# Working image by image, with convolution, projections and second layer issued in small steps between the pieces of a selective scan, and half of the C products on GpSimd

## The chip, the cores and the metric

The kernel runs on one core of a Trainium2 chip. The metric is the time of one execution on the device in microseconds, lower is better. Executions of one kernel agree within about 0.3 %. All runs quoted here were undisturbed ("fast").

## The reference, cut to what matters

The input is four images of 64 x 64 positions with 96 channels, in fp32. Layer 0 is a convolution block with binary weights and a selective scan in four directions; layer 1 is linear attention and a feed-forward net with quantised values.

```
x  = x + layer0(groupnorm(x))
     # 96 -> 192+192 channels (x, z), 3x3 convolution, silu, four scan directions of 192 channels x 16 states:
     dA = exp(dt[..., None] * A)                     # the "decay"
     h  = dA * h + (dt * u)[..., None] * Bt          # the recurrence; (dt*u)*B is the "inject"
     y  = einsum('bkdn,bkn->bkd', h, Ct)             # "C product" and sum over the 16 states
     # four directions added, layernorm over channels, gated by z, projected back to 96
t  = tokens(x)
t  = t + attention(layernorm(t))                     # no softmax: k and v reduce to one small matrix
t  = t + ffn(layernorm(t))                           # 96 -> 384 -> 96, fp8 products
```

## The kernel before

Two images form a pair. For each pair the kernel runs a front (`prologue`: input projection, convolution, projections of B, C and dt), then the scans, then a back (`epilogue`: directions, layernorm, gate). The second layer comes at the very end. Only the softplus of dt (`prepare`) runs between the scans.

```
    for pr in range(NB // 2):
        ...
            prologue(tc, a, pr, gT, c)
            scans(tc, pr, gT, c)
        epilogue(tc, a, pr, c)
    layer1(tc, a, x1d, out, ident, eps5, hmask)
```

The scans of all images are 1536 pieces of 128 rows (32 channels x 4 states) by 1024 positions. A piece passes through five operations on four engines: a decay on ScalarE (into PSUM), an inject on GpSimd, the scan on VectorE, the C product on GpSimd or VectorE, and a reduction on TensorE (four matmuls in the trace) that sums over the states into a PSUM bank `y`.

```
        bcp, dlp, sw, pw, yw = pool("sbc", 6), pool("sdl", 3), pool("sw", 8), pool("spw", 2), pool("syw", 2)
        ps_a, ps_b = pool("sps", 2, space=PSUM), pool("spb", 2, space=PSUM)
        ...
        def pooled(i):
            return i % 8 in (0, 3, 5)
        ...
        def scan(i):
            ...
            h = w if pooled(i) else dA
            nc.vector.tensor_tensor_scan(
                h, dA, w, 0.0 if ci == 0 else carries[u][:, g, q : q + 1], ALU.mult, ALU.add
            )
            if pooled(i):
                carry(i, h)                                   # a ScalarE copy of the last column
                nc.gpsimd.tensor_tensor(w, h, cr, ALU.mult)
            else:
                nc.vector.tensor_tensor(w, h, cr, ALU.mult)
                carry(i, h)
        ...
        for i, (u, ci, g, q) in enumerate(pieces):
            ...
            decay(i + 1)
            inject(i + AHEAD)                                 # AHEAD = 4
            scan(i)
            if i % 8 == 2 and i > 8:
                evacuate(i - 3)                               # copies the bank of eight sums out
            if i >= 1:
                reduce(i - 1)
            ...
            advance()                                         # one step of softplus
```

## Time and profile before

The kernel takes 7612.65 us (median of the four runs on one chip, 7603.54 to 7622.04). The lines of its profile are shown and added up in the prediction below. In the list of costliest groups, a line gives the source line, the engine, the operation, what it writes and reads, the count, then total busy time and mean nanoseconds of one, and last the idle time just before it with what ended it. The outcome: 5093 us of the profiled execution are scans with two full engines, and 2492 us are other work in which those two engines have little to do.

### The profile page before, as it was taken

What the parts mean: (1) busy time and instruction counts of PE and PEld (TensorE: products, weight loads), DVE (VectorE), ACT (ScalarE), POOL (GpSimd) and SP (SyncE); (2) the same over time, 40 slices, a digit from 0 to 9 for tenths busy, and PEclk for the clock granted to TensorE, in tenths of its full rate; (3) what the DMA queues carried; (4) which work ended last, traced back from release to release, by engine and by line L of the source; (5) the groups of instructions that cost most, each with busy time, mean ns of one, the idle gap of its engine ahead of it and who ended that gap; (6) DMA issues with size and microseconds to landing.
All of it is one profiled execution on the core that took longest, in us unless ns stands there. A gap on an engine that the chain in (4) does not pass through costs nothing. (4 is left out here: it accounts for less than half of the span.)

```text
span 7584.7 us, 48672 instructions
## 1 busy us (share of the span) xinstructions
PE 4209.9 (56%) x14531; PEld 1204.3 (16%) x14531; DVE 5865.7 (77%) x4026; ACT 3108.1 (41%) x4634; POOL 5004.0 (66%) x2226
## 2 busy tenths in 40 slices
PE   4996455555555444435799455555555544442756
PEld 2233100000000000002324210000000000000344
DVE  1112799999999999987212299999999999996877
ACT  2124455555554433422313355555555444441323
POOL 0000799999999999950000099999999999993012
PEclk8557556666666666657558566666655566665867
DMA  2001566654666444443100356655567544445111
GB/s 49 33 17 63 186 187 168 184 184 165 186 179 166 158 144 154 142 182 83 44 34 9 124 175 179 180 175 184 181 168 179 171 155 147 151 148 192 47 25 32
DMA packets 750581, 1010.17 MB, mean 133 GB/s; under 512 B 521875, under 2 KB 522444, under 8 KB 743756
## 3 DMA queue, kind: packets, MB, share of 16 engines
q1 hardware_dynamic: 750316, 1007.07, 44.1%
q8 instruction: 114, 1.87, 0.1%
q14 instruction: 151, 1.24, 0.1%
HBM read 812.17 MB, written 188.48 MB: 132 GB/s over the span
## 5 line engine op out<-in xcount | busy, mean ns | idle before, releaser
L524 POOL TENSOR_TENSOR w<-dl,bc 128x1024 f32<-128x1024 f32 x1536 | 3584.3, 2373 | 1360.7 <-DMA dl<-dld 1291.3
L561 PE MATMUL yp<-w,sum 128*32 128x512 f32 x6144 | 2417.8, 985 | 2584.7 <-POOL w L546 2379.8
L516 ACT ACTIVATE dA<-dl,anm 128x1024 f32<-128x1024 f32 x1536 | 1715.6, 1117 | 667.7 <-DVE w L548 474.7
L541 DVE TENSOR_TENSOR_SCAN dA<-dA,carry,w 128x1024 f32<-128x1024 f32 x720 | 1688.1, 2345 | 62.4 <-ACT dA L516 31.3
L546 POOL TENSOR_TENSOR w<-w,bc 128x1024 f32<-128x1024 f32 x576 | 1362.4, 2366 | 132.3 <-ACT carry L533 107.8
L548 DVE TENSOR_TENSOR w<-dA,bc 128x1024 f32<-128x1024 f32 x960 | 1176.0, 1225 | 83.8 <-DVE dA L541 1.4
L561 PEld LDWEIGHTS yp<-w,sum 128*32 128x32 f32 x6144 | 351.9, 146 | 4422.9 <-POOL w L546 3155.7
L541 DVE TENSOR_TENSOR_SCAN w<-dA,carry,w 128x1024 f32<-128x1024 f32 x432 | 1011.3, 2341 | 0.0
L533 ACT COPY carry<-dA 128x1 f32<-128x1 f32 x720 | 114.7, 159 | 1666.5 <-DVE w L548 1666.5
L541 DVE TENSOR_TENSOR_SCAN dA<-dA,w 128x1024 f32<-128x1024 f32 x240 | 548.8, 2287 | 32.5 <-ACT dA L516 19.2
L311 DVE TENSOR_SCALAR t<-t,pv 128x512 f32<-128x512 f32 x48 | 23.3, 486 | 610.8 <-ACT t L307 610.8
L541 DVE TENSOR_TENSOR_SCAN w<-dA,w 128x1024 f32<-128x1024 f32 x144 | 328.3, 2280 | 48.5 <-POOL w L524 48.0
L296 PE MATMUL cvps<-tp,cw 128*128 128x512 bf16 (+1 forms) x576 | 358.0, 622 | 2.5 <-ACT u L275 2.5
L299 PE MATMUL cvps<-tp,cw 64*128 64x512 bf16 (+1 forms) x576 | 356.5, 619 | 0.0
L269 POOL MEMSET tp<- 128x4356 bf16 x6 | 22.1, 3726 | 485.3 <-ACT xsT L257 485.3
L651 PE MATMUL mu<-y,lnm 128*128 128x512 f32 x224 | 137.5, 756 | 272.8 <-DVE y L645 227.6
L356 DVE COPY xr<-tp 64x1536 bf16<-64x1536 bf16 x64 | 60.8, 949 | 293.9 <-PE tp L351 293.9
L775 POOL MEMSET tT<- 1x4096 f32 x4 | 14.0, 3506 | 406.1 <-PE zp L704 296.9
L442 PE MATMUL dps<-gT,wdz 48*128 48x64 bf16 (+1 forms) x2048 | 175.8, 310 | 92.7 <-ACT pd L464 91.7
L307 ACT ACTIVATE t<-cvps,cbias,csc 128x512 f32<-128x512 f32 x48 | 37.3, 777 | 443.3 <-PE cvps L299 443.3
L457 DVE TENSOR_TENSOR pd<-dps,pu 128x512 f32<-128x512 f32 x192 | 165.1, 860 | 55.2 <-DMA pu<-ud 47.1
L819 POOL CAST h<-h 128x512 fp8e5<-128x512 f16 x96 | 81.9, 867 | 190.0 <-DVE h L818 190.0
(174 smaller groups left out, 4329.2 us busy)
## 6 DMA issues: line engine op xcount, KB each, us to landing
dl<-dld SPq DMA_DIRECT2D x768, 512.0 KB
bc<-bcd SPq DMA_DIRECT2D x512, 512.0 KB
dld<-pd SPq DMA_DIRECT2D x64, 1024.0 KB
pu<-ud SPq DMA_DIRECT2D x96, 512.0 KB
yd<-ys SPq DMA_DIRECT2D x384, 128.0 KB
dld<-pd SPq DMA_DIRECT2D x64, 512.0 KB
yk<-yd SPq DMA_DIRECT2D x12, 2048.0 KB
ud<-u SPq DMA_DIRECT2D x12, 1024.0 KB
```

The costliest lines, as they stand in the source:

```text
L296: nc.tensor.matmul(ps[prow, :], c["cw0"][:, t, co], tpad[j][:, win[0], win[1]], start=(t == 0), stop=False)
L299: nc.tensor.matmul(ps[prow, :], c["cw1"][rows, t, co], tpad[2][rows, win[0], win[1]], start=False, stop=(t == 8),)
L442: nc.tensor.matmul(pv[rows, s], c["wdz"][:, k, s, ch], gT[:, k, h, :, c0 : c0 + 16], start=True, stop=True)
L457: nc.vector.tensor_tensor(d[:, 1, cols].rearrange("p (i j) -> p i j", j=64), ps.rearrange("p (i j) -> p i j", j=64), uv[:, 8 * hf : 8 * hf ...
L516: nc.scalar.activation(t, dlt[u, ci, g][0], AF.Exp, scale=c["anm"][:, units[u][0], g, q : q + 1])
L524: nc.gpsimd.tensor_tensor(t, dlt[u, ci, g][1], bct[u, ci, q][0], ALU.mult)
L533: nc.scalar.copy(carries[u][:, g, q : q + 1], h[:, CH - 1 : CH])
L541: nc.vector.tensor_tensor_scan(h, dA, w, 0.0 if ci == 0 else carries[u][:, g, q : q + 1], ALU.mult, ALU.add)
L546: nc.gpsimd.tensor_tensor(w, h, cr, ALU.mult)
L548: nc.vector.tensor_tensor(w, h, cr, ALU.mult)
L561: nc.tensor.matmul(y[at : at + 32, :], c["sum4"], prod[:, 512 * hf : 512 * hf + 512], start=(q == 0), stop=(q == NQ - 1), tile_position=(0 ...
L651: nc.tensor.matmul(ps, c["lnm"][:, m, :], src[s], start=(i == 0), stop=(i == len(terms[T]) - 1))
```

## The change

The intent is to let the 2492 us of other work run on TensorE and ScalarE while VectorE and GpSimd scan. For that the images are worked one at a time, all other stages are rewritten with channels on the partitions and cut into small generator steps, and one such step is issued per piece. Only the first image's front and the last image's back stay outside. To give VectorE room for the new steps, GpSimd takes half the C products in place of three in eight, and copies the carry of its own pieces. The diff is a rewrite of most of the file; its core:

```
+    def back():
+        yield from prologue(c, 1)
+        for b in range(NB):
+            if b + 2 < NB:
+                yield from prologue(c, b + 2)
+            while not scans[b].done(2):
+                yield
+            yield from turn(c, b)                  # sums of the two transposed directions
+            while not scans[b].done(NK):
+                yield
+            yield from epilogue(c, b)              # back of layer 0, and all of layer 1
...
-        bcp, dlp, sw, pw, yw = pool("sbc", 6), pool("sdl", 3), pool("sw", 8), ...
-        ps_a, ps_b = pool("sps", 2, space=PSUM), pool("spb", 2, space=PSUM)
+        gT=pool("gTp", 2), bc=pool("bcp", 5), dl=pool("dlp", 3), w=pool("wp", 7), y=pool("yp", 2),
+        dA=pool("dAp", 2, space=PSUM), ps=pool("psp", 1, space=PSUM),     # single banks for all sums
...
-            return i % 8 in (0, 3, 5)
+        return i % 2 == 0
...
+        if pool:
+            if ci < NCH - 1:
+                nc.gpsimd.tensor_copy(one, h[:, CH - 1 : CH])
+            nc.gpsimd.tensor_tensor(w, h, cr, ALU.mult)
...
+            if i >= 1:
+                self.reduce(i - 1)                 # still ahead of the step, as before
...
+            interleave(lanes)                      # one step of softplus
+            next(back, None)                       # one step of everything else
```

## The prediction

> **What bounds the kernel now.** I first read the occupancy in forty slices, because it shows whether the kernel is one regime or several.
>
> ```profile
> PE   4996455555555444435799455555555544442756
> DVE  1112799999999999987212299999999999996877
> POOL 0000799999999999950000099999999999993012
> ```
>
> The reader is to see two long stretches in which VectorE (DVE) and GpSimd (POOL) are both at 9, and three stretches (start, middle, end) in which GpSimd does nothing and VectorE little. TensorE is full only in two spots there. Next, the first and last scan instruction give the borders: scans run from 792 to 3338 us and from 4344 to 6891 us. Busy time by stretch then says what each regime is limited by (columns: stretch, length, busy us of PE, weight loads, DVE, ACT, POOL, TensorE clock, DMA share, GB/s):
>
> ```profile
> 171.00:560.00 389.00, 376.54 (x952) 102.87 (x952) 62.64 (x93) 74.43 (x93) 0.00 (x0) 0.54 0.07 25
> 792.00:3327.00 2535.00, 1261.61 (x3938) 230.58 (x3940) 2436.11 (x1412) 1213.53 (x1858) 2432.96 (x1053) 0.63 0.55 166
> 4300.00:6900.00 2600.00, 1287.27 (x4016) 236.72 (x4015) 2452.16 (x1427) 1229.92 (x1883) 2441.41 (x1056) 0.62 0.56 167
> 7100.00:7585.00 485.00, 307.93 (x1734) 206.43 (x1732) 363.06 (x509) 146.13 (x230) 95.86 (x100) 0.74 0.15 36
> ```
>
> So 2546 + 2547 = **5093 us are scans**, 1536 pieces at 3.32 us, with VectorE and GpSimd both 96% busy. The other 7585 - 5093 = **2492 us** are convolution, projections, normalisation and the second layer: 792 at the start, 1006 in the middle, 694 at the end, with the two scan engines mostly empty. The costliest groups give the price of a piece:
>
> ```profile
> L524 POOL TENSOR_TENSOR w<-dl,bc 128x1024 f32<-128x1024 f32 x1536 | 3584.3, 2373 | 1360.7 <-DMA dl<-dld 1291.3
> L561 PE MATMUL yp<-w,sum 128*32 128x512 f32 x6144 | 2417.8, 985 | 2584.7 <-POOL w L546 2379.8
> L516 ACT ACTIVATE dA<-dl,anm 128x1024 f32<-128x1024 f32 x1536 | 1715.6, 1117 | 667.7 <-DVE w L548 474.7
> L541 DVE TENSOR_TENSOR_SCAN dA<-dA,carry,w 128x1024 f32<-128x1024 f32 x720 | 1688.1, 2345 | 62.4 <-ACT dA L516 31.3
> L546 POOL TENSOR_TENSOR w<-w,bc 128x1024 f32<-128x1024 f32 x576 | 1362.4, 2366 | 132.3 <-ACT carry L533 107.8
> L548 DVE TENSOR_TENSOR w<-dA,bc 128x1024 f32<-128x1024 f32 x960 | 1176.0, 1225 | 83.8 <-DVE dA L541 1.4
> ```
>
> Of eight pieces three have their C product on GpSimd. GpSimd: 8 x 2.37 + 3 x 2.37 = 26.1 us, 3.26 a piece; VectorE: 8 x 2.34 + 5 x 1.225 = 24.9 us, 3.11 a piece, plus the softplus stage that runs between the scans (0.68 + 0.86 us x 192, 0.19 a piece) = 3.30. Both give the measured 3.32. Inside the scans GpSimd's own waits are small; the whole-run list of its waits has these:
>
> ```profile
> POOL w L524 <- DMA dl<-dld: 1291.3, 2, 648.3
> POOL w L546 <- ACT carry L533: 107.8, 122, 3.2
> POOL w L524 <- DMA bc<-bcd: 66.2, 55, 5.1
> ```
>
> The first is no DMA problem: two waits of 648 us, the stages ahead of each scan.
>
> **What the Trainium skill says.** "Perfetto Trace Analysis", Optimization Strategy: where the most-contended engine differs between regimes, interleaving the regimes can help. The slices above show such regimes, and the change does this. "GPSIMD Engine Reference", 3.1: a two-input elementwise operation costs GpSimd about 2.6 cycles per element at 1.2 GHz, some twice VectorE; 1024 elements would be 2.2 us, the trace has 2.37 against 1.225, so it agrees. "TensorE: Matmul & The Clock Gate", Engine queue depths: ScalarE, VectorE and GpSimd are strict FIFOs, and only weight loads overtake on TensorE. No row of this trace tests that, but it is what makes me charge for interleaving. The same page, on fp8: without the double-row mode it runs at bf16 speed; I therefore count no gain for the convolution's fp8. (The fp8 matmuls before, 0.47 us for 96x512 at another clock, do not contradict it.)
>
> **The change part by part.**
>
> *1. Only image 0's front and image 3's back stay outside.* The order of instructions says so: on VectorE 205 rows stand ahead of the first scan and 90 after the last; on GpSimd nothing but two products follows the last inject. The background generator takes one step per piece. I counted its steps: front 183, transposing two directions' sums 34, back 218. Fronts 1 and 2 fill pieces 0 to 366, image 0's back ends at piece 618, image 1's at 1053, image 2's at 1370; all this the VectorE order confirms. Image 3's back, 218 steps, can only start after piece 1536.
>
> *Start.* Constants and input until the convolution: 171 us before for two images, about 150 for one. Convolution: 16 tiles, each 18 matmuls x 0.615 us (L296/L299 at clock 0.5) = 11.1, one projection 0.5, two ScalarE reads of the single bank 1.55, so 13.2 x 16 = 211. Then 64 units of 12 transposes (0.106 each, busy time over count), a ScalarE copy (half of 1.59), six matmuls (0.16) and hand-overs: 3.3 x 64 = 211, plus 16 x 2.3 for signs and B/C = 37. Round trips through memory 25, eight softplus steps (92 us for twelve before) 60. Sum **about 695 us**, against 792: halving the images saves little because the new steps use single banks and run one after the other.
>
> *Tail.* First half of image 3's back, per 512 tokens: 22 fp32 matmuls of 1.0 us (L651: 244 us for 224), some two not on the path, other small matmuls 4, about a dozen ScalarE/VectorE steps of 0.65 us on the path 8, loads of 2 MB at some 190 GB/s 10: 42 us, x 8 = 336. Second half: 3 fp32 matmuls, fp8 matmuls, ten steps, load latency: 20 us x 8 = 160. **About 500 us**, against 694.
>
> *2. Half the C products on GpSimd.* GpSimd: 1536 + 768 = 2304 products. Back-to-back triples of injects in the timeline last 6.95 us, so 2.32 each: 5345 us. New are 576 carry copies of 128x1 on GpSimd (its 128x1 fills take 0.11 us; I take 0.2): 115. Sum **5460 us, 3.55 a piece, against 3.26**. VectorE: 1536 x 2.34 + 768 x 1.225 = 4535, plus softplus 256 x 1.5 = 390 and about 330 of other steps = 5255, 3.42 a piece. GpSimd becomes the bound. The carry wait (108 us) goes.
>
> *3. What interleaving costs in the scans.* (a) Convolution, 48 tiles: a tile takes four pieces, 4 x 3.55 = 14.2 us, but TensorE needs 11 + 0.5 + 4 x 1.57 (2417.8/1536 for the reductions) = 17.8 us, and the next decay queues on ScalarE behind a read that waits for it: about 4.5 us each, 215. (b) Back, first half, 24 blocks: TensorE 28 + 14 x 1.57 = 50 us in 14 pieces worth 50 us, unevenly spread: 6 each, 145. (c) Transposing units: 3.8 us of TensorE against 3.55: 0.4 x 200 = 80. (d) B/C buffers 6 to 5: the load for the second next tile goes out one piece later; waits for it from 66 to perhaps 200. Sum 640, of which a third should overlap: **+425 us**.
>
> Total: 695 + 5460 + 425 + 500 = **7080 us**.
>
> **The rivals.**
> *Everything hides.* Steps fall wholly into TensorE's and ScalarE's slack (TensorE is 50% busy in the scans, ScalarE 48%). Then 695 + 5460 + 500 = 6655. For it: before, softplus hid almost fully. Against it: the convolution stretch shows TensorE 97% busy for 389 us; that doesn't fit into half an engine without delay.
> *TensorE becomes the bound.* Its work in the scans sums to some 4600 us (2418 reductions, 540 convolution, 840 back, 800 the rest) of 5900, so not on average; but if each phase lost twice my charge (3a to 3d in full, doubled), the scans take 6700 and the total nears 7900: slower. Against it: reductions lag with four injects ahead and seven w buffers.
> *More work on GpSimd is itself a loss.* If GpSimd's copies cost 0.5 us and its products lengthen beside more VectorE traffic, 3.8 a piece, total 7450: no change within 2%.
>
> **Range and chances.** The sure gain is 2492 - 1195 = 1297 us of serial work; the sure cost is 367 us of scan bound; the unsure cost is 0 to 1200. For a gain below 2% the unsure cost must pass 800, nearly twice my estimate. Range 6750 to 7440; faster 0.85, same 0.10, slower 0.05.
>
> **What the changed profile would show.** First scan near 695, last near 6580. GpSimd at 9 in all slices between, product at 2.3 to 2.4 us, x768, carry copies near 0.2; if much above, step 2 is wrong. GpSimd's waits for the B/C load near 200 us (3d). Scans per us lower in the two convolution phases (pieces 30 to 100 and 215 to 285) than in pieces 1404 to 1536, which have only scans and should run at 3.6. TensorE about 75% in the scans. A tail of 450 to 550 us with no engine full. I would be wrong if phases show VectorE waiting on decays for most of the time, if the tail is memory-latency bound at 700, or if the products slow down.

## The result, and the profile after

The changed kernel is correct and takes 7545.59 us (median of four, 7530.09 to 7555.51). The ratio to the kernel before is 0.991 (95 % interval 0.9888 to 0.9932). A ratio here is the mean time of one kernel's fast runs over that of the other's fast runs of the same rounds, so it is not quite the ratio of the medians. The gain is 0.9 %, and the prediction had 7 %.

Busy tenths in forty slices of the kernel after:

```profile
PE   3745678767976776566777677556557765654684
DVE  1106786788676779988757677988867789888401
POOL 0007787888787778898868778888988789999500
```

The empty stretch in the middle is gone, as intended. But GpSimd now stands at 7 and 8 where it stood at 9, and VectorE falls to 5 and 6 in places. Only near the end, where no background is left, it stays at 9.

Busy time by stretch (columns as in the prediction: stretch, length, busy us of PE, weight loads, DVE, ACT, POOL, TensorE clock, DMA share, GB/s), for the scans and the tail:

```profile
597.00:7083.00 6486.00, 4342.56 (x15056) 1355.04 (x15058) 5126.24 (x3211) 3391.29 (x4985) 5455.16 (x2904) 0.69 0.55 156
7083.00:7548.00 465.00, 320.24 (x640) 117.02 (x636) 49.71 (x89) 118.62 (x203) 0.00 (x0) 0.66 0.21 52
```

Start 597, scans 6486, tail 465. The start was predicted at 695 and the tail at 500, so both came out better. The scans were predicted at 5460 + 425 = 5885. They are 601 us longer, which is more than the whole miss of 466 us. GpSimd is 84 % busy in them (5455 of 6486 us).

The groups that answer to those of before:

```profile
L849 POOL TENSOR_TENSOR w<-dl,bc 128x1024 f32<-128x1024 f32 x1536 | 3594.7, 2356 | 1319.6 <-DMA dl<-dld 586.8
L883 PE MATMUL yp<-w,sum 128*32 128x512 f32 x6144 | 2331.0, 873 | 1692.3 <-POOL w L868 1119.1
...
L868 POOL TENSOR_TENSOR w<-w,bc 128x1024 f32<-128x1024 f32 x768 | 1804.6, 2350 | 110.1 <-DVE w L864 62.2
L864 DVE TENSOR_TENSOR_SCAN dA<-dA,carry,w 128x1024 f32<-128x1024 f32 x576 | 1351.5, 2346 | 356.9 <-ACT dA L842 242.5
```

No operation of the scan became slower: injects 2356 ns (2373 before), C products 2350 (2366), scans 2346 (2345). What grew is idle time. This scan group waited 356.9 us in 576 pieces; before, the like group waited 62.4 us in 720. The list of waits says on whom (engine, tile, line, what it waits for, total us, times, longest):

```profile
PE yp L883 <- POOL w L868: 1119.1, 339, 33.5
...
ACT carry L872 <- DVE w L870: 882.0, 372, 9.4
...
POOL w L849 <- PE yp L883: 401.6, 190, 11.8
DVE dA L864 <- ACT dA L842: 372.6, 206, 10.8
DVE w L864 <- ACT carry L872: 329.0, 136, 11.7
...
POOL w L849 <- DMA bc<-bcd: 310.9, 87, 15.4
```

GpSimd is the bound engine, so the loss is read from its own waits. Beside the two above, its list has these:

```profile
POOL w L849 <- DMA dl<-dld: 586.8, 4, 509.8
...
POOL carry L867 <- DVE w L864: 105.4, 94, 4.2
...
POOL w L868 <- DVE w L864: 62.2, 52, 6.3
```

Inside the scans that makes 402 us for TensorE to free a buffer, 311 for B and C, 168 for VectorE's scans, 77 for the loads of dt and dt * u (586.8 less the first wait of 509.8, ahead of all scans), and 48 between its own carry copy and product (110.1 - 62.2 in the line of L868). The sum is 1006 us, nearly all of the 1026 us by which 6486 exceeds the predicted bound of 5460.

The waits form a circle: TensorE waits for GpSimd's product, ScalarE for VectorE, VectorE for ScalarE, GpSimd for TensorE. In the kernel before, waits of TensorE and ScalarE were long too, but cost nothing, because VectorE and GpSimd waited for nobody for long. Now both do. The timeline of 10 us in the second transposing phase shows one turn of the circle (start us, duration, engine, line; in brackets the idle time before and what ended it):

```profile
1896.74 2.35 POOL L868 TENSOR_TENSOR w<-w,bc 128x1024 f32<-128x1024 f32 x1
...
1899.33 1.92 PE L883 MATMUL yp<-w,sum 128*32 128x512 f32 x4 [2.46 <-POOL w L868]
...
1901.80 0.84 PE L452 MATMUL acc<-xr,wlT_dt 64*32 64x256 bf16 x3
...
1902.68 0.37 ACT L462 CAST ibc<-acc 128x256 bf16<-128x256 f32 x1 [3.45 <-PE acc L452]
1902.95 0.57 ACT L464 ACTIVATE sgn<-acc,sld 128x256 bf16<-128x256 f32 x1
...
1904.15 1.11 ACT L842 ACTIVATE dA<-dl,anm 128x1024 f32<-128x1024 f32 x1
...
1905.36 2.29 DVE L864 TENSOR_TENSOR_SCAN w<-dA,w 128x1024 f32<-128x1024 f32 x1 [2.99 <-ACT carry L872]
```

Follow it downwards. GpSimd's product ends at 1899.09. The reduction that needs it is at the head of TensorE's queue, so TensorE had done nothing for 2.46 us, although the background's matmuls behind it in the queue needed nothing from GpSimd. They end only at 1902.6. ScalarE's next entry reads their sums and had waited 3.45 us. The next decay sits behind it in ScalarE's queue and runs at 1904.15. VectorE had stood still for 2.99 us when its scan starts. The list puts this wait down to the carry copy, but this scan reads no carry, and it starts 0.10 us after the end of its decay (1905.26). All 136 waits of scans that are put down to that copy end 0.10 us or (once) 0.45 us after the scan's own decay, so they are waits for decays.

The spot shows the links of the circle and not their usual size. In the three transposing phases TensorE waits for such products for only 11 to 12 us each, because it is 83 to 94 % busy there. It is 45 to 52 us in a convolution phase, 26 to 43 in the first half of a back and 77 to 88 in the second. In the pieces without background such waits are long as well (206 us in 115 pieces) and cost nothing.

From the starts of the scans in the trace I took the pace of each phase. The excess is over 3.56 us a piece, which is the GpSimd bound that the prediction worked out:

| background phase | pieces | us a piece | excess, us | charged in the prediction |
|---|---|---|---|---|
| convolution (3 images) | 195 | 4.62, 4.16, 4.10 | 143 | 215 |
| transposing units (3) | 207 | 4.61, 4.76, 4.86 | 245 | 80 |
| back, first half (3) | 340 | 4.60, 4.50, 4.51 | 331 | 145 |
| back, second half (3) | 314 | 4.03, 4.05, 3.93 | 139 | none |
| turning the directions (4) | 136 | 4.37, 4.25, 4.28, 3.73 | 83 | none |
| other front parts | 147 | 3.4 to 4.3 | 63 | none |
| no background | 191 | 3.85 with softplus, 3.52 without | 14 | none |

### The profile page after: what moved, and what is told of

The parts are those of the page before. It is cut to its first block, busy times and chain, and to the rows that moved or that the text cites. A ratio compares the mean times of both kernels' runs of the same rounds, so it can differ in the third digit from the quotient of the medians.

```text
span 7548.3 us, 57482 instructions
## 1 busy us (share of the span) xinstructions
PE 4965.0 (66%) x17443; PEld 1665.5 (22%) x17443; DVE 5249.6 (70%) x3505; ACT 3712.7 (49%) x5506; POOL 5462.7 (72%) x2921
## 5 line engine op out<-in xcount | busy, mean ns | idle before, releaser
L849 POOL TENSOR_TENSOR w<-dl,bc 128x1024 f32<-128x1024 f32 x1536 | 3594.7, 2356 | 1319.6 <-DMA dl<-dld 586.8
L842 ACT ACTIVATE dA<-dl,anm 128x1024 f32<-128x1024 f32 x1536 | 1703.5, 1112 | 458.2 <-DVE w L870 203.0
L868 POOL TENSOR_TENSOR w<-w,bc 128x1024 f32<-128x1024 f32 x768 | 1804.6, 2350 | 110.1 <-DVE w L864 62.2
L864 DVE TENSOR_TENSOR_SCAN dA<-dA,carry,w 128x1024 f32<-128x1024 f32 x576 | 1351.5, 2346 | 356.9 <-ACT dA L842 242.5
L864 DVE TENSOR_TENSOR_SCAN w<-dA,carry,w 128x1024 f32<-128x1024 f32 x576 | 1349.2, 2342 | 302.3 <-ACT carry L872 209.6
L870 DVE TENSOR_TENSOR w<-dA,bc 128x1024 f32<-128x1024 f32 x768 | 940.8, 1225 | 46.1 <-DVE dA L864 1.4
L788 PE MATMUL dps<-gT,wdz 48*96 48x64 bf16 x2048 | 219.7, 293 | 226.0 <-DMA gT<-gTd 175.5
L404 PE MATMUL cv<-tp,cw 96*96 96x512 fp8e5 x1152 | 321.1, 442 | 17.0 <-ACT r L415 16.8
L482 PE MATMUL tp<-identb,xg 64*64 64x64 bf16 x3072 | 303.9, 265 | 4.5 <-ACT xr L488 3.4
L556 PE MATMUL ys<-ey,ident 96*96 96x512 f32 x384 | 246.6, 787 | 86.8 <-DMA ey<-yd 83.3
L482 PEld LDWEIGHTS <-xg 64*64 64x64 bf16 x3072 | 268.2, 173 | 127.1 <-issue 122.8
L801 DVE TENSOR_TENSOR pd<-dps,pu 96x512 f32<-96x512 f32 x256 | 219.1, 856 | 53.8 <-DMA pu<-ud 37.8
```

The source lines that it names most:

```text
L404: nc.tensor.matmul(ps, c.cw[:, j, t, 96 * h : 96 * h + 96], tpad[j][:, 8 * q + dy : 8 * q + dy + 8, dx : dx + IW], start=(j == 0 and t == ...
L482: nc.tensor.transpose(tp[:, 64 * j : 64 * j + 64], src, identb[rows, rows])
L556: nc.tensor.matmul(ps, w, x, start=(i == 0), stop=(i == len(pairs) - 1))
L788: nc.tensor.matmul(pv[:, s], c.wdz[:, k, s, 96 * h : 96 * h + 96], gT[:, :, c0 : c0 + 16], start=True, stop=True)
L801: nc.vector.tensor_tensor(d[:, 1].rearrange("p (i j) -> p i j", j=64), ps.rearrange("p (i j) -> p i j", j=64), uv[:, 8 * hf : 8 * hf + 8], ...
L842: c.nc.scalar.activation(t, self.dlt[e, ci, g][0], AF.Exp, scale=c.anm[:, KORD[e], g, q : q + 1])
```

## The experiments

The theory that I came to (C, where an expectation uses letters; A puts the loss into the interleaving as such, B into TensorE being too full) was the order in TensorE's queue: the reduction waits for a late product at its head, and everything behind it waits in turn. The rivals were that TensorE's work itself is the bound, that blocks of 18 convolution matmuls are, that B/C buffers or the single bank `y` are, and that half the C products on GpSimd are. Each run was measured beside the kernel before on the same chip. To set a run against the kernel after I take the difference of their ratios times 7605 us (0.01 is 76 us); the interval of one ratio is 11 to 23 us on either side (30 for e1, which ran twice), so a difference of two is uncertain by some 17 to 28 us.

**e1_serial.** The changed kernel with nothing interleaved: fronts and backs run between the images' scans.

```
-    for _ in prologue(c, 0):
-        pass
+    for b in range(NB):
+        for _ in prologue(c, b):
+            pass
+        scans[b].run(iter(()), None)
+        for _ in turn(c, b):
+            pass
+        for _ in epilogue(c, b):
+            pass
+    return
```

> The same instructions, but no stage between the scan tiles: each image's front, its scans, the turn and its back one after the other. Theory A (the added time in the scans comes from the steps that stand between the tiles): the scans fall from 4.22 to 3.5 to 3.6 us a piece, some 5480 us, and the whole takes 60 + 4 x 535 (fronts) + 5480 + 4 x 560 (turn and back), near 9900 us. Rival (the scans themselves have become slower, by GpSimd's larger share and five B/C buffers): they stay near 4.2 a piece and the whole takes near 10900 us.

Measured: 9793.28 us, ratio 1.2896. The scans alone take 3.70 us a piece, 5690 us in all. The gaps between the images are 996, 998 and 994 us. So interleaving hides 2988 us of serial work, and lengthens the scans by 6486 - 5690 = 796 us. Two more facts come out. First, the rewritten stages are much longer when run alone: 597 + 2988 + 516 = 4101 us, against 2492 us before. The rewrite into small steps with single banks and one image at a time costs 1609 us of serial time, and what was interleaved was this larger amount. Second, even the scans alone miss 5460 us by 230, and GpSimd's only long wait inside them accounts for it:

```profile
POOL w L856 <- DMA bc<-bcd: 229.9, 66, 9.1
```

That is the prediction's 3d ("from 66 to perhaps 200") and it was right.

**e2_pecut.** Three of four reductions write only 64 of 512 columns. The sums are wrong (the comparison with the reference still passed its tolerance); every instruction and every wait stays.

```
+        n = 512 if q == 0 else 64
-                y[at : at + 32, :], c.sum4, prod[:, 512 * hf : 512 * hf + 512],
+                y[at : at + 32, 0 : n], c.sum4, prod[:, 512 * hf : 512 * hf + n],
```

> Wrong result on purpose: of the four accumulating reductions of a group, three stream 64 columns in place of 512, so TensorE's work for a piece falls from about 1.5 us to about 0.6; nothing else changes. Theory B (TensorE, in order and too full in the transposing, convolution and back phases, is what delays the scans): at least half of the 1010 us excess goes, 6900 to 7050 us. Rival (ScalarE's order and the B/C loads delay them, TensorE's fill is incidental): less than 150 us goes, 7400 to 7550 us.

Measured: 7420.15 us, ratio 0.977, so 106 us below the kernel after. TensorE's amount of work counts, but shortening three of four reductions gave only a tenth of the 1026 us by which the scans exceed 5460. Two things belong to this number. By the starts of the scans, the three transposing phases, where TensorE is full, became 117 us shorter, and the three convolution phases 3 us. And the granted clock fell from 0.69 to 0.59 with the shorter reductions, the convolution's matmuls taking 376 us in place of 321; so the run shows less than TensorE's work is worth.

**e3_bc6.** Six B/C buffers, as before the change.

```
-        ... bc=pool("bcp", 5), ...
+        ... bc=pool("bcp", 6), ...
```

> Six B/C buffers again in place of five, nothing else. If GpSimd's 311 us of waits for B/C loads are on the path, 150 to 300 us go: 7250 to 7400 us. If TensorE is what holds the pieces (theory B), GpSimd waits for reductions instead, and less than 80 us go: 7470 us or more.

Measured: 7494.51 us, ratio 0.9872, 29 us below. GpSimd's wait for B and C falls from 310.9 to 267.8 us only. The sixth buffer is a small part, at the edge of the noise.

**e4_evac1.** The copy of the single `y` bank comes one piece earlier, so that the next sum finds the bank free earlier.

```
-            if i % 8 == 2 and i > 8:
-                self.evacuate(i - 3)
+            if i % 8 == 1 and i > 8:
+                self.evacuate(i - 2)
```

> The evacuation of the single y bank is issued one piece earlier, ahead of the first reduction of the next group. TensorE waits 197 us for that evacuation now. Theory B: TensorE's waits delay everything queued behind, so 80 to 200 us go: 7350 to 7470 us. Rival (the wait is absorbed by the seven w buffers): no change within 40 us.

Measured: 7420.27 us, ratio 0.9766, 110 us below. The single bank is a link of the circle: GpSimd's wait for TensorE falls from 401.6 to 231.9 us.

**e5_lag2.** The reduction follows its product two pieces later in place of one, with an eighth `w` buffer.

```
-            if i >= 1:
-                self.reduce(i - 1)
+            if i >= 2:
+                self.reduce(i - 2)
```

> The reduction of a piece is issued two pieces after its scan in place of one, with eight w buffers so that GpSimd's injects have the same room; by this the evacuation also stands ahead of the next group's first reduction, which alone gave 103 us. Theory C (a reduction at the head of TensorE's queue waits for a product on GpSimd, 1119 us in all; the step's matmuls stand behind it, ScalarE's next operation of the step waits for them, the next decay stands behind that, and VectorE waits for the decay): 300 to 500 us go in all, 7050 to 7230 us, and VectorE's waits for decays and carries, 796 us after the change, fall by half. Rival (TensorE's own work or ScalarE's): not below 7380 us.

Measured: 7291.93 us, ratio 0.9588, 245 us below the kernel after. The later reduction also comes behind the evacuation, which is e4's gain, so this run alone doesn't single out the order.

**e6_order.** Only the place of one call changes. The reduction is issued after the background's step in place of before it.

```
             self.scan(i)
-            if i >= 1:
-                self.reduce(i - 1)
             ...
             interleave(lanes)
             next(back, None)
+            if i >= 1:
+                self.reduce(i - 1)
```

> The same idea without a buffer: the reduction of the last piece is issued after the background step of this piece, not ahead of it. Theory C: the step's matmuls get ahead of the wait, 150 to 350 us go, 7180 to 7380 us. Rival: the wait only moves to the next step, less than 60 us.

Measured: 7308.93 us, ratio 0.9602, 234 us below. No instruction, no buffer and no dependency changed, only the order in TensorE's queue. This shows theory C: the product that is late no longer holds up work that doesn't need it. The waits of e6, to be set beside those of the kernel after:

```profile
DVE dA L864 <- ACT dA L842: 417.6, 213, 12.0
POOL w L849 <- PE yp L883: 304.2, 162, 9.7
DVE w L864 <- ACT carry L872: 187.9, 100, 11.6
```

```profile
POOL w L868 <- DVE w L864: 17.7, 12, 6.4
...
POOL carry L867 <- DVE w L864: 8.0, 6, 2.6
```

GpSimd's wait for TensorE fell from 402 to 304 us and its wait for VectorE's scans from 168 to 26, together 240 us, which is the gain. Both of VectorE's lines are waits for decays (see the timeline above). With the scans into `w` that the list itself gives to the decay (94.6 us in the kernel after, 46.5 here) they fell from 796 to 652 us. So this order is one cause, not the only one.

**e7_split.** The 18 matmuls of a convolution tile in two steps of nine.

```
                     for j in range(2):
                         for t in range(9):
                             ...
+                        if j == 0:
+                            yield
```

> The 18 convolution matmuls of a tile in two steps of nine, 48 more steps in the scans, nothing else. If the block of 18 (8 to 11 us of TensorE) delays the decays, most of the 143 us excess of the three convolution phases goes: 7390 to 7450 us, and 4.1 to 4.6 us a piece there fall below 4.0. If not, no change within 40 us.

Measured: 7536.07 us, ratio 0.9902: no change. The block of 18 is no cause. A matmul of it took 0.28 us (321.1 us for 1152), so a block is 5.0 us and not the 11 of the prediction.

**e8_pool38.** The old fraction of C products, three in eight, in the changed kernel.

```
-        return i % 2 == 0
+        return i % 8 in (0, 3, 5)
```

> Three of eight C products on GpSimd again, in place of half. If GpSimd's own work sets the pace (the step of my prediction): about 0.29 us a piece less for GpSimd, but VectorE then has 3.1 + 0.5 us a piece, so about 100 us go, 7420 us. Under theory C fewer reductions wait for GpSimd's late products, 150 to 300 us go, 7220 to 7370 us. If VectorE was near its limit: slower, 7600 us or more.

Measured: 7662.11 us, ratio 1.0069, 121 us slower than the kernel after. In the last pieces, which have no background, it does run faster (3.21 us a piece against 3.52), so GpSimd's bound is lower there as step 2 says. Elsewhere it loses. Its waits show where:

```profile
POOL w L849 <- PE yp L883: 752.6, 258, 8.8
```

GpSimd with less to do only waits longer for the reductions to free its buffers. That VectorE then has 192 more products of 1.225 us beside the background's steps fits this; the run doesn't separate it.

**e12_before_half.** The other way round: the kernel before, with half the C products on GpSimd and nothing else.

```
-            return i % 8 in (0, 3, 5)
+            return i % 2 == 0
```

> The kernel before with half of the C products on GpSimd, the rest untouched: this part of the change alone. By my prediction's step 2 GpSimd needs 3.55 us a piece (its carry copies stay on ScalarE) and is the bound: scans 5093 to about 5450 us, 7940 to 7990 us in all. If VectorE was the bound of the scans before: no change or a little faster, 7500 to 7620 us.

Measured: 7821.69 us, ratio 1.03, so 228 us above the kernel before. The figure of 3.55 us a piece in my expectation was a slip: it holds the carry copies on GpSimd, which this kernel doesn't have. From the prediction's own spacing of 2.32 us, 2304 products take 5345 us, 252 more than the 5093 us of before; 228 were measured. In the scans' middle 2000 us, GpSimd's injects of this run and, in the second fence, of the kernel before:

```profile
L524 POOL TENSOR_TENSOR w<-dl,bc 128x1024 f32<-128x1024 f32 x578 | 1348.5, 2360 | 1.8 <-DMA bc<-bcd 1.7
```

```profile
L524 POOL TENSOR_TENSOR w<-dl,bc 128x1024 f32<-128x1024 f32 x607 | 1412.0, 2352 | 23.1 <-DMA bc<-bcd 20.5 <-PE yp L561 2.5
```

In 2000 us 578 pieces pass in place of 607 (3.46 us each against 3.29), and GpSimd's injects wait for 1.8 us in all. Step 2's bound is shown. Alone this part of the change costs 228 us; inside the interleaved kernel e8 shows it saves 121.

**e9_combo.** Reduction after the step (e6), earlier evacuation (e4), six B/C buffers (e3) and eight `w` buffers (e5) together.

> The repairs together: the reduction after the background step, the evacuation one piece earlier, six B/C buffers, eight w buffers; the result stays right. Under theory C the gains mostly add, as each removes another wait of TensorE or GpSimd: 7120 to 7220 us. If they all relieve the same wait: no better than the reduction's order alone, 7290 us.

Measured: 7318.69 us, ratio 0.9632. This is no better than e6 alone (0.9602). The expectation that these gains add was wrong. I read this so that e4's 110 us and e6's 234 us are gains on the same circle of waits, which needs opening only once; the runs show only that the gains don't add.

**e11_combo_pecut.** e9 with the reductions cut as in e2 (wrong sums).

> The repaired version with three of four reductions cut to 64 columns (wrong sums on purpose). It says what is left to TensorE's own work once the queue order is mended: over 150 us less than the repaired version if theory B holds for the rest, under 60 us if not.

Measured: 7090.67 us, ratio 0.9331, 229 us below e9, where the same cut was worth 106 us in the kernel after. So TensorE's own amount of work counts for more once the queue order is mended (the clock fell here too, from 0.69 to 0.60).

**e10_spread.** e9, with an idle step after every second transposing unit of the background, so that these phases last longer and TensorE gets fewer matmuls per piece.

```
                         yield
+                    if k % 2:
+                        yield
```

> The run before with one idle step after every second transposing unit (96 more steps, inside the 132 pieces that stand alone at the end). If TensorE's fill in the three transposing phases (90% busy, 4.4 to 4.9 us a piece) is a limit of its own: their excess of some 60 us each shrinks to 20, about 80 to 120 us less than without. If only waits matter: within 30 us of it.

Measured: 7188.91 us, ratio 0.9467, 125 us below e9.

**e13_spread_only.** The same edit in the kernel after, with nothing else.

> Kernel after with one edit: an idle step after every second transposing unit of the background, queue order and buffers untouched. It tells the crowding of TensorE in the transposing phases from the order of its queue. If crowding is a cause of its own: 7545 minus 100 to 130, so 7415 to 7445 us. If spreading only pays once the reduction no longer stands at the head of TensorE's queue: 7500 us or more.

Measured: 7469.65 us, ratio 0.9832, 59 us below the kernel after: between the two expectations. Crowding of TensorE in the transposing phases is a cause of its own. To relieve it pays less while the queue order is bad: 59 us here, 125 on top of e9, 83 on top of e6 (next run).

**e14_order_spread.** The kernel after with e6's and e10's edits alone.

> Kernel after with two edits: the reduction issued after the background step, and the idle step after every second transposing unit; no further buffers, no moved evacuation. If the sixth B/C buffer, the eighth w buffer and the moved evacuation add nothing beyond these two: 7180 to 7200 us, as the version with all five edits (7189). If they are worth something beside them: 7220 to 7260 us.

Measured: 7211.31 us, ratio 0.9493, 83 us below e6 and between the two expectations. All five edits together (e10) reach 0.9467. So the additional buffers and the moved evacuation are worth 20 us beside these two edits, about what the intervals leave open.

**e15_order_spread_carry.** e10 with the carry copies of odd pieces on VectorE in place of ScalarE.

```
-                nc.scalar.copy(one, h[:, CH - 1 : CH])
+                nc.vector.tensor_copy(one, h[:, CH - 1 : CH])
```

> The version of 7189 us with the carry copies of odd pieces moved from ScalarE to VectorE. ScalarE's longest wait there is at that copy, for VectorE's scan or product (1054 us), and what is queued behind it on ScalarE (evacuations of the background's single banks, the next decay) waits with it. If this wait holds the rest of the excess: 6950 to 7080 us, with the scans' waits for decays falling from 521 to below 300 us. If it is slack of an engine that is only 50 per cent busy: 7180 to 7260 us, the 672 copies on VectorE (0.1 to 0.15 us each) being the only effect.

Measured: 7089.1 us (7073.82 to 7101.23), ratio 0.9332, 103 us below e10; it is correct. This fits the expectation that ScalarE's wait at that copy was harmful, as what is queued behind it came late; the run also takes the 576 copies themselves (0.16 us each) off ScalarE and doesn't separate the two. VectorE pays 576 copies of 0.15 us for it (the 672 of the expectation was a miscount). The second half of my expectation failed, as the scan's wait for decays hardly fell, from 521 to 479 us (from 632 to 579 with the waits put down to carry copies and those of the scans into `w`):

```profile
DVE dA L866 <- ACT dA L844: 478.8, 159, 11.8
ACT dA L844 <- DVE carry L874: 433.8, 265, 3.4
```

The first is the longest wait that remains in VectorE's scans. This is the fastest correct version, 6.7 % below the kernel before and 5.8 % below the kernel after.

**e16_decay_lead.** e14 with three decay buffers in SBUF in place of two in PSUM, and the decay issued two pieces ahead.

```
-        dA=pool("dAp", 2, space=PSUM), ps=pool("psp", 1, space=PSUM),
+        dA=pool("dAp", 3), ps=pool("psp", 1, space=PSUM),
...
-            if i + 1 < n:
-                self.decay(i + 1)
+            if i + 2 < n:
+                self.decay(i + 2)
```

> The version with reduction order and spread alone, with three decay buffers in SBUF in place of two in PSUM and the decay issued two pieces ahead in place of one. If the short lead of the decay is what hands every delay of ScalarE on to the scan: 200 us or more below the version with order and spread alone on the same chip (about 7000 us), and the scan's waits for decays below 200 us. If TensorE's and the background's own work is the rest: within 60 us of it. A third outcome: decays in SBUF lengthen scan or exponential beside GpSimd (then their durations, 2.34 and 1.12 us, rise, and the run is slower).

Measured: 10548.57 us, ratio 1.3889: the third outcome, and a drastic one. Groups of this run:

```profile
L851 POOL TENSOR_TENSOR w<-dl,bc 128x1024 f32<-128x1024 f32 x1536 | 5538.6, 3623 | 795.1 <-DMA dl<-dld 591.3
...
L866 DVE TENSOR_TENSOR_SCAN dA<-dA,carry,w 128x1024 f32<-128x1024 f32 x576 | 2160.5, 3751 | 252.1 <-POOL w L851 245.0
...
L872 DVE TENSOR_TENSOR w<-dA,bc 128x1024 f32<-128x1024 f32 x768 | 2129.2, 2772 | 52.1 <-DVE dA L866 0.9
...
L869 POOL COPY carry<-w 128x1 f32<-128x1 f32 x576 | 1134.6, 1970 | 2.2 <-DVE w L866 2.2
```

Every operation of the scan on VectorE and GpSimd lengthened: scan 2346 to 3751 ns, VectorE's product 1225 to 2772, the inject 2356 to 3623, a carry copy of one column from 192 to 1970. ScalarE's decay hardly did (1112 to 1146), and a softplus step on VectorE with one input in PSUM did not (856 to 855). The Trainium skill states the mechanism in "SBUF — State Buffer", Who interferes with whom: a VectorE instruction with two inputs in SBUF contends with a GpSimd instruction that reads SBUF, and with at most one, outside the two-port modes, it doesn't. With the decays in PSUM the scan and VectorE's product have one SBUF input each; here they have two. The trace agrees. So it is the PSUM decay buffer that lets the two engines of the scan run side by side. Whether a longer lead of the decay would help stays open: no kernel here tried a third decay buffer in PSUM.

## Why the prediction was wrong, point by point

**Start (695) and tail (500): right in kind, too high in size.** They measured 597 and 465. The convolution at the start was the over-charge that could be named: its 18 matmuls took 4.1 us there in place of 11.1, at a granted clock of 1.00 where the convolution before had 0.54.

**Step 2, the bound of GpSimd: right.** 5460 us or 3.55 a piece was predicted. The pieces without background at the end ran at 3.52, the carry copies took 192 ns (0.2 was assumed), and e12 shows the bound in the old kernel without any other change. Products and scans did not lengthen, so the third rival fell.

**Step 3d, B/C buffers: right** for the scans alone (230 us of waits in e1). In the interleaved kernel the sixth buffer gave back only 29 us of 311 us of waits. What else delays those loads was not settled. One rival stands untested: all loads and stores are issued from SyncE, in one queue, whose entries also wait for others (1464.4 us for the copies of the sums on ScalarE in the kernel after), and the background's stores stand in it too.

**Step 3, the cost of interleaving (+425 us): the step that failed.** It measured 6486 - 5460 = 1026 us. On GpSimd, the bound engine, these are 402 us of waiting for TensorE, 311 for B/C loads (charged 200), 168 for VectorE's scans, and smaller ones. The prediction charged the work of TensorE that exceeds the pace, and not the waits that the order in the queues adds. By phases, the term was mis-sized in three ways.
- The transposing units (3c) were charged 80 us and cost 245. The kind was right, as TensorE is over the pace there. The size was not: a piece holds 4.1 to 4.4 us of TensorE's work in place of 3.8, against a pace of 3.56, which over some 204 pieces is about 135 us by my estimate; the rest of the 245 isn't split. (The sum itself has a slip: 3.8 - 3.55 is 0.25 and not 0.4.) In the first of these phases the granted clock was 0.55, with 0.87 in the same stage before; whether that lengthened the work isn't shown:

```profile
1037.00:1356.00 319.00, 283.63 (x1515) 132.19 (x1516) 221.66 (x132) 181.01 (x279) 245.71 (x137) 0.55 0.45 128
```

```profile
560.00:700.00 140.00, 115.07 (x757) 67.23 (x756) 33.09 (x43) 59.42 (x45) 0.00 (x0) 0.87 0.09 33
```

- The first half of the back (3b) was charged 145 and cost 331, and its second half and the turning of directions were charged nothing and cost 222. In neither half of the back is TensorE's sum of work over the pace on average (3.3 to 3.4 us a piece in the first, 2.3 in the second). They pay the circle of waits: e6 removed 91 us in the first halves and 37 in the second with the order alone.
- "A third should overlap" had no ground. The phases follow each other in time, so their charges add. Only the charge for the convolution (215 against 143) was too high, and its reason did not hold: a block of 18 took 5.0 us and not 11, TensorE is 63 to 67 % busy there, and e7 changed nothing.

**What the prediction did not see** is that moving work under the scans ties four in-order queues into one circle. It named strict FIFOs, and used them only for one read of ScalarE in step 3a. It did not ask what stands at the head of TensorE's queue in every piece. The runs put sizes on it and on the crowding beside it, in this order of adding: 234 us for the order (e6), 83 more for the crowding (e14), 20 for buffers and evacuation (e10), 103 for the carry copies on ScalarE (e15). That is 440 of 1026 us; e9 shows that another order of adding would share it out differently. Another part is TensorE's amount of work (229 us in e11 against e9), which overlaps with the crowding. In e15 the scans run from 599 to 6622 us, so some 560 us are left above the bound, which GpSimd's list gives to B/C loads (187 us), to VectorE's scans (145) and to TensorE (99) for the most part; why these stay is not settled.

**The rivals.** "TensorE becomes the bound" with phases that lose twice the charge came closest for the scans: it doubled 640 to 1280 us, where 1026 were measured. As a mechanism it is right for the transposing phases, which gave e2's 117 us, and not for the others, where the order counts (e6). The total came closest to that of "More work on GpSimd is itself a loss" (7450), by luck: neither did the products lengthen nor did the copies take 0.5 us. "Everything hides" was wrong. The conditions under which I would be wrong held one that came true in kind: VectorE waiting on decays, 372.6 + 329.0 + 94.6 = 796 us in the list of waits, though not "for most of the time". As a sign it is weak: in e1, where GpSimd waits for B/C loads alone, VectorE waits for decays for 542 us.

**Where the expected gain went.** Of 2492 us outside the scans before, 1062 are left (597 + 465), a gain of 1430. The scans grew from 5093 to 6486 us, a loss of 1393: 367 for GpSimd's higher bound and 1026 for waits. The two profiled runs, 7584.7 and 7548.3 us, differ by what is left of this, 36 us.

## What to carry to other kernels

When background work goes under a loop that is already bound by two engines, ask for every in-order queue what stands ahead of the new work and whether it can be late; put what waits for another engine behind what waits for nothing, which here was worth 234 us for one moved call. Add the charges of phases that follow one another, and charge the rewritten work and not the old: here the stages cut into small steps were 1609 us longer when run alone. An operand in PSUM can be what lets VectorE and GpSimd run together, so a buffer should not be moved out of it for the sake of depth without one look on the chip.

## What the Trainium skill lacked or had wrong

- "Perfetto Trace Analysis", Optimization Strategy, speaks for interleaving regimes with different busiest engines, and lacks its price: hiding 2988 us lengthened the loop by 796 us (e1), and moving one call gave 234 us back (e6).
- "TensorE: Matmul & The Clock Gate", Part 1, says that activity releases the throttle. The convolution before had TensorE 97 % busy for 389 us at a granted clock of 0.54; the same stage at the start of the kernel after, 80 % busy for 92 us, had 1.00. Part 4 has it that transposes don't count as busy in the same way; the transposing phase after agrees (0.55), but the stage before, also full of transposes, ran at 0.87. The runs don't say what sets the clock.
- "SBUF — State Buffer", Who interferes with whom, has the rule that e16 ran into, and calls the shared port pair an exclusive lock. No page has sizes for a scan: 2346 to 3751 ns beside GpSimd's 2356 to 3623 ns, for the same tiles of 128 x 1024 in fp32.
